# A two-layer graph kernel on one core: another order of work at the head, at the tail and in layer 1's first groups

## The chip, the core and the metric

The kernel runs on one core of a Trainium2 chip. The metric is the device time of the program in microseconds, as the median of several runs. One core has a matrix engine (TensorE, PE in the profile, with its weight loads as PEld), and three engines that work on tiles elementwise: VectorE (DVE), ScalarE (ACT) and GpSimd (POOL). SyncE (SP) issues most DMA transfers. Every engine has its own queue of instructions and takes them in program order; semaphores make one engine wait for another.

## The reference

All tensors are fp32; `x` is (64, 256, 512), that is 64 batches of 256 nodes with 512 features, and `adj` is (256, 256).

```python
def _layernorm(x):                     # no scale, no shift, eps 1e-5
    return (x - mean(x)) / sqrt(var(x) + 1e-5)

# layer 0
h = maximum(_layernorm(x), 0)
x = x + einsum('nm,bmd->bnd', adj, h) @ W0 + b0
# layer 1
h = maximum(_layernorm(x), 0)
q, k, v = (h @ W + b for W, b in ((Wq, bq), (Wk, bk), (Wv, bv)))    # 8 heads of 64
scores = q . k / 8 + (1 - adj) * -1e9                                # per batch and head, 256 x 256
out = softmax(scores) . v
x = x + out @ Wo + bo
```

## The kernel before

**Groups and layers.** The 64 batches are 32 groups of two. Layer 0 runs over all groups first (about 43 to 605 us of the profiled execution) and leaves the residual x and the transposed hidden tensor of every group in DRAM. Layer 1 runs over the groups again (about 605 to 2630 us, some 62 us for a group).

**Seven products for eight.** A matrix product is cut into 2x2 blocks and made with seven block products in Strassen's way (Winograd's form). Each operand needs four sums of blocks: on the weight side s1 to s4, on the data side t1 to t4 (`Halves.sums`, L483, on POOL: t1 = b12-b11, t3 = b22-b12, t2 = b22-t1, t4 = b21-t2). `project` is the one-level form: seven steps with the products a11.b11 (bank pa), a12.b21 (pb), s2.t2 (pa), s3.t3 (pc), s1.t1 (pa), a22.t4 (pc) and s4.b22 (pa). DVE adds the banks into the result (`add`, L802). Layer 0 uses it, and so do groups 0 and 1 of layer 1. From `FIRST2 = 2` on layer 1 uses `quartered`, in which most of the seven products (named A to G) are cut once more into seven. That needs sums of the sums: of the weights once (`block_sums`, which puts 128x128 sums of some 0.3 to 0.5 us on DVE or POOL, spread over ticks), of the data in each group (`Blocks.sums`, L582, on POOL).

**The order is written by hand.** A scheduler does not choose: instructions go into the engines' queues in the order in which the Python code emits them. A counter of ticks stands in for time. `after(delay, fn)` puts work off until `tick()` has been called so many times, and `run(gen, steps)` takes steps from a generator and ticks after each. `quartered` only makes a table of named steps, and an order string (QK, VO, V1, O1, OL) says how they follow: a token is the matrix (q, k, v, o), the product (A to G) and the step. Small letters are matmuls, copies and adds of one product; `oEk` is a matmul of wo's E and `oEl` the add after it. `|` is a tick, and `x` emits the next waiting exponent. QK makes q and k, VO makes v of the next group and the output of this one. V1 makes v alone and is used for groups 2 and 31; O1 makes the output of group 30, beside group 31's attention, and OL that of group 31.

**Layer 0's parts.** `ready(g, ...)` makes h: `moments` on DVE (L42, L43), `norm_scales` on POOL (L51 to L54: epsilon, power -1/2, and nb = -mean times it), relu on ACT (L830) with rs and nb as scale and bias. `turn_adjacency` transposes the adjacency: DVE copies it to another order of rows (adj_p, L362), PE transposes (L367), DVE copies the result to adjT. `first_adjacency` is group 0's adj.h in plain products (py, L856), copied by ACT to yT (L864) with POOL's t sums of `YH[0]` behind the copies; `adjacency(g)` is that of the other groups in the one-level form (py_a, py_b, py_c at L907, copies on ACT such as L926). It needs sums of adjT (`adjacency_sums`) and of h (`feature_sums`, L891, and `last_feature_sum`, L894, on POOL). `layer0(g)` multiplies by W0 (w_0a and so on, L490), adds to x, and makes the hidden tensor. `weight_sums` (L458) makes s1 to s4 of a weight.

**Layer 1's parts.** A seed is a copy by ACT of a bias or mask into a PSUM bank, on which PE then accumulates (`bank(seed=...)`, L291): the score banks are seeded with the mask, the output banks with the bias. `score` emits two seeded and two unseeded pairs of banks for each half of the heads; DVE reads them (L1126 seeded, L1129 unseeded), for the unseeded ones the row maximum is subtracted on POOL (L1136) or DVE (L1134), ACT takes the exponent in place (L1152), and POOL adds each pair of key tiles (`key_sum`, L1159). `attend` makes the denominators from those sums (pden, L1168) and attention times v (pav, L1175). The denominator is copied (L1182) and inverted by two ACT and three POOL instructions (L1189 to L1193), and in the last attention by DVE's reciprocal (L1197). `divide` (L1211) follows one tick later, then the t sums of the output and `block_outputs`. q and k leave PSUM by ACT copies (L1044). `outputs` issues the DMA of a finished batch (L1084), or in the last group of a quarter (L1082).

**The head and the tail.** The head is emitted as `ready(0)`, `load(1)`, `ready(1)`, a tick, `turn_adjacency`, sums of W0, and `first_adjacency`, of which three steps run before layer 0's seeds. At the tail of group 31 stand in this order: `attend(31, 0)`, `score(31, 1)`, six segments of O1, `attend(31, 1)`, the rest of O1, and OL.

Of the kernel before, what the change touches and what calls it, by code (L numbers as in the profile page):

```python
# [8 lines left out]
F32 = mybir.dt.float32  # L9
# [4 lines left out]
P = 128  # L14
# [31 lines left out]
def norm_scales(nc, pool, mhalf, mv, name):  # L46
# [8 lines left out]
    return rs, nb  # L55


def general_path(tc, x, adj, w0, b0, wq, bq, wk, bk, wv, bv, wo, bo, out):
# [157 lines left out]
    "vFa vA0 vFb vA1 vFc vFd x vA2 | vA3 vGa vFe vBa vp00 vBb vFf vGb | vCa vBc vFi vFg vCb vGc x vBd vFh vFj vCc "  # L216
    "vFl vEa | vBe vGd vEb vCd vGe vBf vCe vEc vCf vBn vGf vBg vEd vFk vGg | vCg vEe vBh vGh vp10 vBi vEf2 vBj x "
    "vCh vCi vDa vBk vGi | vDb vGj vp11 vGk vCj vGl vCk vEf x vDc vDd vm11 vDi | vDj vEg vDe vDk vDf vEi vCl vEj "
    "vEk vm10 vDg vEl0 | vEh vEl1 vDh vEl2 ")
O1 = (  # L220
    "oAz oCi oCj oCk oA0 oBz oA1 x oFa | oB0 oCa oFb oA2 oFc x oA3 | oFd op00 oB1 oFe oEa oCl0 oFf oFi oFg oFj | "
    "oEb oFk oCb oB2 oFh oFl oCc x oB3 op10 oEc | oEd oDa op11 oCd oG0 oCe oDb oG1 oCf oG2 | oEe x oEf oDc oG3 "
    "oCl1 oDi om11 oDj oDd | oCg oDe oEg oDf oDk oEi oCh oEj om10 oEk oDg | oEl oDh oEh ")
OL = (
    "oAz oBz oA0 oA1 oA2 | oA3 oB0 oB1 oFa op00 | oCi oFb oCa oCj oCb oCk oFc oCl0 oFd oEa oFe oCc | oCl1 oCd oEb "
    "oFf oCe oFi oCf oFg oFj oFk oEc oFh oCg oFl oEd | oDa oB2 op10 oB3 oDb oEe oG0 oCh oDc | op11 oDd oG1 oDe "
    "oG2 oDf oEf oG3 oDg | om11 oDi oDj oDk oDh oEg oEi om10 oEj oEk oEh | oEl ")
# [3 lines left out]
def kernel(  # L231
# [127 lines left out]
    def turn_adjacency():  # L359
        adj_p = tmp.tile([P, NT, N], F32, tag="u", name="adj_p")  # L360
        for u in range(NT):
            nc.vector.tensor_copy(adj_p[:, u, :].rearrange("p (t i b) -> p i t b", i=NI, t=NT),  # L362
                                  adj_r[:, u, :].rearrange("p (i t b) -> p i t b", i=NI, t=NT))
# [5 lines left out]
        nc.vector.tensor_copy(adjT, pa)  # L369
# [180 lines left out]
    def block_sums(n):  # L550

        todo = []
        for x in SMALL[n]:
# [5 lines left out]
            eng = nc.vector if x in "BFG" else nc.gpsimd  # L559
# [24 lines left out]
    def quartered(g, n, halves, blocks, by_token, place, first, seeds=None, multiplied=None, done=None):  # L584
# [160 lines left out]
        def more(name, b, i, k):  # L745
            step(name, lambda: add(place(i, k), banks[b], place(i, k)), b, quadrant=(i, k))
# [30 lines left out]
        if first is None:  # L777
            more("El", "pa", 0, 1)
# [35 lines left out]

    def ready(g, moments_at, scales_at, relus_at, batches=1):
# [7 lines left out]
        def scales(i):  # L823
            h.append(norm_scales(nc, small, mhalf, mv[:, i * n:(i + 1) * n, :], f"0_{g}_{i}"))
            if i == 0:
                H0[g] = act.tile([P, T, D], F32, tag="h", name=f"h_{g}", bufs=2)
# [20 lines left out]
    def first_adjacency():  # L847
# [4 lines left out]
        def part(d, b):  # L852
            if d not in pss:
                pss[d] = bank([P, GN], f"py_{d}")
            for k in range(NT):
# [3 lines left out]
        for d in range(DC):  # L859
            part(d, 0)  # L860
        for d in range(DC):
# [5 lines left out]
            if d == 3:  # L867
                YH[0].sums(nc.gpsimd, ("t3", "t4"))
# [13 lines left out]
    def feature_sums(g):  # L882
# [6 lines left out]
        for o, p, q, op in ((s12[:, 0], block(2, 1), block(2, 2), ALU.add), (s12[:, 1], s12[:, 0], block(1, 1), ALU.subtract),  # L889
                            (block(2, 1), block(1, 1), block(2, 1), ALU.subtract)):  # L890
            nc.gpsimd.tensor_tensor(o, p, q, op=op)  # L891
# [133 lines left out]
    def block_outputs(g, step):  # L1025
# [4 lines left out]
        if g == NG - 1:  # L1030
            both.sums(nc.vector)
# [42 lines left out]
    def outputs(g):  # L1074
# [4 lines left out]
        def done(i, k):  # L1079
            complete.append(k)  # L1080
            if g == NG - 1:
# [6 lines left out]
    def plain_outputs(g):  # L1088
        seeds = seed_outputs(g)
# [10 lines left out]
    def score(g, qd, sum_delay=5, exps=(3, 4, 5, 8)):  # L1100
# [4 lines left out]
        def banks(c, b, **how):  # L1105
            return [bank([P, NT * N], f"sc_{g}_{qd}_{c}{b}_{j}", **how) for j in range(2)]

        masked = {cb: banks(*cb, seed=maskT_f, times=1.0 / SCALE) for cb in ((0, 0), (0, 1))}
        while behind_seeds:
            behind_seeds.pop(0)()  # L1110
        for c in range(2):
            for b in range(GB):
                seen = (c, b) in masked
                ps = masked[c, b] if seen else banks(c, b)
# [46 lines left out]
    def attend(g, qd):  # L1161
# [47 lines left out]
        def divide():  # L1209
# [12 lines left out]
            if qd and g >= FIRST2:  # L1222
                block_outputs(g, 1)
# [186 lines left out]
```

## Time and profile before

| what | us |
|---|---|
| median of 3 runs | 2631.18 |
| the 3 runs | 2628.93 to 2632.58 |
| the profiled execution: its time | 2632.4 |
| its span, from the first to the last instruction | 2630.2 |
| busy in the span: PE | 2588.6 (98%) |
| PE weight loads | 2301.6 (88%) |
| POOL | 2075.6 (79%) |
| DVE | 1909.8 (73%) |
| ACT | 1379.4 (52%) |

A busy row is the sum of an engine's instructions in the profiled execution. The page cuts the span into 40 slices of 65.8 us, and PE's row there shows 7 in the first and the last slice and 9 in all between. The granted clock, PEclk, is the speed of TensorE as a part of its full speed; its mean over the span is 0.997. A busy microsecond at clock 0.50 does half a microsecond's work. A matmul of fp32 is a row with "f32" behind its tile, and "out<-in" gives the tiles by the program's names.

### The profile page before, as it was taken

Reading aid. Unit: us, or ns where it says so; the run is one execution under the profiler, and the core shown is the slowest. Engines: PE = TensorE matmul, PEld = TensorE weight load, DVE = VectorE, ACT = ScalarE, POOL = GpSimd, SP = SyncE. Lnnn points to the kernel's source line nnn. Section 1 sums busy time; section 2 is a strip of 40 time slices with the busy share of each in tenths; the row PEclk is TensorE's granted clock in tenths of the full one; section 3 lists DMA queues with packets and bytes.
Section 4 is the critical chain, followed back from the end, with each engine's and each line's share of the span. In section 5 each row is a group of like instructions: output and inputs, shape, how many; then the busy total and the mean of one; then the engine's idle time right before and its main releaser. Section 6 shows DMA issues by size and latency. Waiting matters only on the chain. (4 is left out here: it accounts for less than half of the span.)

```text
span 2630.2 us, 57376 instructions
## 1 busy us (share of the span) xinstructions
PE 2588.6 (98%) x21876; PEld 2301.6 (88%) x21876; DVE 1909.8 (73%) x4166; ACT 1379.4 (52%) x3192; POOL 2075.6 (79%) x2256
## 2 busy tenths in 40 slices
PE   7999999999999999999999999999999999999997
PEld 6999899998788888888888888888888888888885
DVE  5878788875476767777777777777767777777776
ACT  3444454543455555555555555555555555555552
POOL 6888887783777888888877888888888888877884
PEclk9999999999999999999999999999999999999998
DMA  5776666664111122211111111111122211111101
GB/s 134 200 194 186 171 165 186 164 165 106 33 49 49 49 65 63 67 50 49 49 49 50 49 49 49 49 49 49 50 67 65 65 49 49 49 49 49 49 34 50
DMA packets 281095, 211.40 MB, mean 80 GB/s; under 512 B 145904, under 2 KB 212976, under 8 KB 280816
## 3 DMA queue, kind: packets, MB, share of 16 engines
q1 hardware_dynamic: 280352, 207.15, 29.7%
q8 instruction: 175, 2.87, 0.4%
q14 instruction: 104, 0.85, 0.1%
q10 hardware_dynamic: 464, 0.52, 0.1%
HBM read 106.96 MB, written 100.66 MB: 79 GB/s over the span
## 5 line engine op out<-in xcount | busy, mean ns | idle before, releaser
L1126 DVE SCALAR_TENSOR_TENSOR a<-sc,top 128x512 f32<-128x512 f32 x256 | 159.1, 684 | 271.6 <-PE sc L1118 259.1
L1136 POOL TENSOR_TENSOR a<-a,top 128x1024 f32<-128x1024 f32 x125 | 293.5, 2369 | 40.3 <-DVE a L1129 40.3
L1159 POOL TENSOR_TENSOR as<-a 128x512 f32<-128x512 f32 x256 | 318.3, 1276 | 5.8 <-ACT a L1152 5.8
L1191 POOL TENSOR_TENSOR as<-as 128x512 f32<-128x512 f32 x63 | 80.2, 1273 | 284.3 <-ACT as L1190 278.9
L1152 ACT ACTIVATE a<-a 128x1024 f32<-128x1024 f32 x256 | 271.7, 1063 | 15.3 <-POOL a L1136 15.3
L1118 PE MATMUL sc<-q,k 64*128 64x256 f32 x2048 | 240.1, 383 | 1.4 <-ACT sc L291 1.4
L1118 PEld LDWEIGHTS sc<-q,k 64*128 64x128 f32 x2048 | 196.7, 186 | 45.4 <-issue 25.1
L1175 PE MATMUL pav<-a,v 128*32 128x256 f32 x4096 | 234.6, 380 | 0.0
L1175 PEld LDWEIGHTS pav<-a,v 128*32 128x32 f32 x4096 | 133.4, 110 | 89.1 <-issue 1.3
L1182 ACT ACTIVATE as<-pden 128x512 f32<-128x512 f32 x64 | 38.3, 599 | 294.6 <-PE pden L1168 294.6
L42 DVE BATCH_NORM_STATS2 st<-x 128x6 f32<-128x512 f32 x256 | 173.1, 676 | 10.3 <-DMA x<-in_x_dram 8.1
L1129 DVE SCALAR_TENSOR_TENSOR a<-sc,maskT 128x512 f32<-128x512 f32 x256 | 158.4, 681 | 0.0
L291 ACT ACTIVATE sc<-maskT 128x512 f32<-128x512 f32 x256 | 137.4, 591 | 0.0
L830 ACT ACTIVATE h<-x,nb,rs 128x512 f32<-128x512 f32 x128 | 93.9, 803 | 76.8 <-POOL nb L54 76.8
L957 ACT ACTIVATE h<-x,nb,rs 128x512 f32<-128x512 f32 x128 | 97.2, 807 | 53.4 <-POOL nb L54 50.2
L891 POOL TENSOR_TENSOR hs<-h 128x512 f32<-128x512 f32 x31 | 39.4, 1270 | 73.8 <-ACT h L830 63.7
L483 POOL TENSOR_TENSOR t_o<-oT,t_o 128x512 f32<-128x512 f32 x63 | 80.5, 1279 | 12.1 <-DVE t_o L483 9.6
L1211 DVE TENSOR_TENSOR oT<-pav,as 128x512 f32<-128x512 f32 x128 | 82.1, 683 | 8.4 <-POOL as L1193 8.4
L582 POOL TENSOR_TENSOR spare<-h1T,spare 128x128 f32<-128x128 f32 x180 | 82.4, 458 | 7.1
L1044 ACT ACTIVATE q<-q_pa,bq_c 128x256 f32<-128x256 f32 (+1 forms) x150 | 61.8, 456 | 48.9 <-PE q_pa L633 36.6
L802 DVE TENSOR_TENSOR x<-o_pa,x 128x512 f32<-128x512 f32 x120 | 82.4, 687 | 6.1 <-PE o_pa L647 4.8
L52 POOL TENSOR_TENSOR rs<-rs,mhalf 128x2 f32<-128x2 f32 (+1 forms) x97 | 80.0, 825 | 8.1
(1639 smaller groups left out, 8736.1 us busy)
## 6 DMA issues: line engine op xcount, KB each, us to landing
x<-in_x_dram SPq DMA_DIRECT2D x256, 128.0 KB, 3.0
residual<-x SPq DMA_DIRECT2D x256, 128.0 KB, 2.4
hidden<-r SPq DMA_DIRECT2D x128, 256.0 KB, 4.4
h1T<-hidden SPq DMA_DIRECT2D x64, 512.0 KB, 7.4
x<-residual SPq DMA_DIRECT2D x32, 1024.0 KB, 7.8
out_dram<-x SPq DMA_DIRECT2D x62, 512.0 KB, 4.1
w_sb<-in_L_gnn_weight_dram SPq DMA_DIRECT2D x1, 1024.0 KB, 7.3
wq_sb<-in_L_gnn_Wq_dram SPq DMA_DIRECT2D x1, 1024.0 KB, 7.5
```

Source lines behind the costliest of these rows:

```text
L42: nc.vector.bn_stats(st, src)
L291: nc.scalar.mul(t, seed, times)
L582: eng.tensor_tensor(self.operand(o), self.operand(p), self.operand(q), op=ALU.subtract)
L830: nc.scalar.activation(H0[g][:, t, :], xt[:, t, :], AF.Relu, bias=nb[:, t % n:t % n + 1], scale=rs[:, t % n:t % n + 1])
L957: nc.scalar.activation(h1[:, k * NT + t, :], xt[:, k * NT + t, :], AF.Relu, bias=nb[:, t:t + 1], scale=rs[:, t:t + 1])
L1118: nc.tensor.matmul(ps[j][:, kt * N:(kt + 1) * N], k[j * HD:(j + 1) * HD, c, kt * P:(kt + 1) * P], q[j * HD:(j + 1) * HD, c, :], start=(kt ...
L1126: nc.vector.scalar_tensor_tensor(o, ps[j].rearrange("p (k n) -> p k n", k=NT), SCALE, top_b[:, 0:NT, :], op0=ALU.mult, op1=ALU.subtract)
L1129: nc.vector.scalar_tensor_tensor(o.rearrange("p k n -> p (k n)"), ps[j], SCALE, maskT_f, op0=ALU.mult, op1=ALU.add)
L1136: nc.gpsimd.tensor_tensor(a, a, top_b, op=ALU.subtract)
L1152: nc.scalar.activation(a, a, AF.Exp)
L1159: nc.gpsimd.tensor_tensor(AS[c, b], a4[:, :, 0, :], a4[:, :, 1, :], op=ALU.add)
L1175: nc.tensor.matmul(po[f][h * 32:(h + 1) * 32, b * N:(b + 1) * N], v[:, k, h * HD + f * 32:h * HD + f * 32 + 32], A[h // 2, b][:, (h % 2) * ...
```

## The change

The arithmetic is the same but for one inversion (below); what differs is where instructions stand, which engine does some of them, and how a few are cut.

1. **Head.** `turn_adjacency` is emitted first, with its copies on ACT. Group 0's h is made tile by tile (`first_ready`): epsilon on DVE and the power on POOL (`power`), nb in one DVE instruction (`shift`), the relu of a tile one tile behind. Group 1 uses `power` and `shift` too, at tick 8 instead of 4, with its relus at 9. `adjacency_sums` moves from tick 4 to 1, and group 1's feature sums from 8 to 9. `first_adjacency` runs over k first for batch 0, and t3 and t4 of `YH[0]` come one tick later. Group 2's relus come at 4 instead of 3.
2. **Feature sums.** In every group of layer 0 the third sum (s3, in place in h) is emitted before the second (s2).
3. **Seeds.** The seeds of group 0's first scores and those of the outputs of groups 0 and 1 are emitted before the last step of the product ahead of them.
4. **Block sums of weights.** wo's are all on POOL, and before wo's F was on DVE; wv's start at tick 3 instead of 2, two to a tick instead of four.
5. **Orders.** V1, O1 and OL are rewritten, and four segments of O1 instead of six stand ahead of `attend(31, 1)`.
6. **Tail.** The output sums of (30, 1) come six ticks later and those of (31, 0) four, behind key sums. Key sums and exponents of group 31 are due at other ticks, and POOL's subtraction in `score(31, 1)` comes three ticks later. In the last attention DVE takes half of the reciprocals and the ACT and POOL form takes the other half. t3, t2 and t4 of the last output are on DVE, both of its block sums on POOL. The last add is in two pieces, and the last quarter leaves by two DMAs, on SP's and ACT's queues.

```diff
+def power(nc, pool, mhalf, mv, name):
+    n = mv.shape[1]
+    rs = pool.tile([P, n], F32, tag="rs", name=f"rs_{name}")
+    nc.vector.tensor_scalar(rs, mv[:, :, 1], EPS, None, op0=ALU.add)
+    nc.gpsimd.tensor_tensor(rs, rs, mhalf[:, :n], op=ALU.pow)
+    return rs
+def shift(nc, pool, mv, rs, name):
+    nb = pool.tile([P, mv.shape[1]], F32, tag="nb", name=f"nb_{name}")
+    nc.vector.scalar_tensor_tensor(nb, mv[:, :, 0], -1.0, rs, op0=ALU.mult, op1=ALU.mult)
+    return nb
XX...
     def turn_adjacency():
-            nc.vector.tensor_copy(adj_p[:, u, :].rearrange("p (t i b) -> p i t b", i=NI, t=NT),
-                                  adj_r[:, u, :].rearrange("p (i t b) -> p i t b", i=NI, t=NT))
+            nc.scalar.copy(adj_p[:, u, :].rearrange("p (t i b) -> p i t b", i=NI, t=NT),
+                           adj_r[:, u, :].rearrange("p (i t b) -> p i t b", i=NI, t=NT))
...
-        nc.vector.tensor_copy(adjT, pa)
+        nc.scalar.copy(adjT, pa)
...
     def block_sums(n):
-            eng = nc.vector if x in "BFG" else nc.gpsimd
+            eng = nc.vector if x in "BFG" and n != "o" else nc.gpsimd
...
-            more("El", "pa", 0, 1)
+            more("El", "pa", 0, 1, 2 if g == NG - 1 else 1)
...
+    def first_ready():
+        xt, mv = X[0], small.tile([P, T, 2], F32, tag="mv", name="mv0_0")
+        H0[0] = act.tile([P, T, D], F32, tag="h", name="h_0", bufs=2)
+        rs = []
+        def relu(t):
+            nb = shift(nc, small, mv[:, t:t + 1, :], rs[t], f"0_0_{t}")
+            nc.scalar.activation(H0[0][:, t, :], xt[:, t, :], AF.Relu, bias=nb, scale=rs[t])
+        for t in range(T):
+            moments(nc, small, mv, t, xt[:, t, :], "0_0")
+            rs.append(power(nc, small, mhalf, mv[:, t:t + 1, :], f"0_0_{t}"))
+            if t:
+                relu(t - 1)
+        relu(T - 1)
...
     def ready(g, moments_at, scales_at, relus_at, batches=1):
-            h.append(norm_scales(nc, small, mhalf, mv[:, i * n:(i + 1) * n, :], f"0_{g}_{i}"))
+            if g == 1:
+                rs = power(nc, small, mhalf, part, name)
+                h.append((rs, shift(nc, small, part, rs, name)))
+            else:
+                h.append(norm_scales(nc, small, mhalf, part, name))
...
     def first_adjacency():
-        for d in range(DC):
-            part(d, 0)
+        for k in range(NT):
+            for d in range(DC):
+                part(d, 0, (k,))
...
-                YH[0].sums(nc.gpsimd, ("t3", "t4"))
+                after(1, YH[0].sums, nc.gpsimd, ("t3", "t4"))
...
     def feature_sums(g):
-        for o, p, q, op in ((s12[:, 0], block(2, 1), block(2, 2), ALU.add), (s12[:, 1], s12[:, 0], block(1, 1), ALU.subtract),
-                            (block(2, 1), block(1, 1), block(2, 1), ALU.subtract)):
+        for o, p, q, op in ((s12[:, 0], block(2, 1), block(2, 2), ALU.add),
+                            (block(2, 1), block(1, 1), block(2, 1), ALU.subtract),
+                            (s12[:, 1], s12[:, 0], block(1, 1), ALU.subtract)):
...
     def block_outputs(g, step):
-            both.sums(nc.vector)
+            both.sums(nc.gpsimd)
...
         def done(i, k):
-            if g == NG - 1:
+            if g == NG - 1 and (i, k) == (0, 1):
+                for t, queue in enumerate((nc.sync, nc.scalar)):
+                    queue.dma_start(quarter_of(out[g * GB + k], i)[:, t], quarter(xt, i, k)[:, t])
+            elif g == NG - 1:
...
+    def score_bank(g, qd, c, b, **how):
+        return [bank([P, NT * N], f"sc_{g}_{qd}_{c}{b}_{j}", **how) for j in range(2)]
+    def score_seeds(g, qd):
+        return {cb: score_bank(g, qd, *cb, seed=maskT_f, times=1.0 / SCALE) for cb in ((0, 0), (0, 1))}
-    def score(g, qd, sum_delay=5, exps=(3, 4, 5, 8)):
+    def score(g, qd, sums=(5, 6, 7, 8), exps=(3, 4, 5, 8), masked=None, top_at=0):
...
+                    elif top_at:
+                        after(top_at, lambda a: nc.gpsimd.tensor_tensor(a, a, top_b, op=ALU.subtract), a)
...
-        def invert():
+        def invert(c=slice(0, GN)):                  # the same five instructions on the columns c
...
         if final:
-            for c in range(4):
+            for c in range(2):
                 nc.vector.reciprocal(rden[:, c * P:(c + 1) * P], den[:, c * P:(c + 1) * P])
+            invert(slice(N, GN))
...
-            if qd == 0:
-                HO[g].sums(nc.gpsimd, ("t1",))
-            elif g < NG - 1:
-                HO[g].sums(nc.gpsimd, ("t3", "t2", "t4"))
+            late = 6 if (g, qd) == (NG - 2, 1) else 4 if (g, qd) == (NG - 1, 0) else 0
+            which = ("t3", "t2", "t4") if qd else ("t1",)
+            if late:
+                after(late, HO[g].sums, nc.gpsimd, which)
             else:
-                HO[g].sums(nc.vector, ("t3", "t2"))
-                HO[g].sums(nc.gpsimd, ("t4",))
+                HO[g].sums(nc.vector if final else nc.gpsimd, which)
             if qd and g >= FIRST2:
-                block_outputs(g, 1)
+                block_outputs(g, late + 1)
...
-    ready(0, (0, 0, 2, 2), (0, 2), (1, 1, 3, 3), batches=2)
+    turn_adjacency()
+    first_ready()
     load(1)
-    ready(1, (4, 4, 4, 4), (4,), (8, 8, 8, 8))
-    after(4, adjacency_sums)
-    after(8, feature_sums, 1)
-    after(8, last_feature_sum, 1)
+    ready(1, (4, 4, 4, 4), (8,), (9, 9, 9, 9))
+    after(1, adjacency_sums)
+    after(9, feature_sums, 1)
+    after(9, last_feature_sum, 1)
     tick()
-    turn_adjacency()
...
-            ready(g + 2, (1, 1, 1, 1), (1,), (3, 3, 3, 3))
+            ready(g + 2, (1, 1, 1, 1), (1,), (3, 3, 3, 3) if g else (4, 4, 4, 4))
...
-    run(plain(0, *second))
-    score(0, 0, 4, (3, 4, 5, 6))
+    second = plain(0, *second)
+    run(second, 6)
+    seeds = score_seeds(0, 0)
+    run(second)
+    score(0, 0, (4, 5, 6, 7), (3, 4, 5, 6), seeds)
...
-            score(g, 1, 3, (3, 4, 5, 6))
+            score(g, 1, (2, 3, 5, 4), (1, 2, 4, 3), top_at=3)
...
-        for n, at in (("q", 7), ("k", 16)) if g == 0 else (("v", 2),) if g == 1 else (("o", 2),) if g == 2 else ():
+        for n, at in (("q", 7), ("k", 16)) if g == 0 else (("v", 3),) if g == 1 else (("o", 2),) if g == 2 else ():
-                after(at + i // 4, *work)
+                after(at + i // (2 if n == "v" else 4), *work)
...
-            run(last, 6)
+            run(last, 4)
...
-            score(g + 1, 0, 5, None if g + 1 >= FIRST2 else (3, 4, 5, 8))
+            score(g + 1, 0, (5, 6, 7, 8) if g + 1 < NG - 1 else (1, 1, 1, 1), None if g + 1 >= FIRST2 else (3, 4, 5, 8))
...
-                run(plain(g + 1, n, halves, *rest))
+                steps = plain(g + 1, n, halves, *rest)
+                run(steps, 5)
+                seeds = seed_outputs(g)
+                run(steps)
                 multiplied()
...
-                    run(follow(steps, V1))
+                    steps = follow(steps, V1)
+                    run(steps, 6)
+                    if g < FIRST2:
+                        seeds = seed_outputs(g)
+                    run(steps)
```

## The prediction, made before the changed kernel ran

> **What bounds the kernel now.** I read the page's slices first, then the windows, then the waits of TensorE (PE), then the timeline around each wait. The windows (us: length, then busy time of PE, weight load, DVE, ACT, POOL, then the granted clock) say where PE is not busy:
>
> ```profile
> 0.00:50.00 50.00, 32.70 (x168) 27.68 (x169) 24.38 (x54) 17.00 (x27) 28.11 (x45) 1.00 0.55 134
> 50.00:600.00 550.00, 550.00 (x3341) 503.76 (x3340) 447.54 (x891) 266.72 (x413) 443.32 (x603) 1.00 0.67 177
> ...
> 640.00:820.00 180.00, 172.58 (x1335) 145.13 (x1334) 106.52 (x207) 84.48 (x195) 132.70 (x145) 0.99 0.20 51
> 820.00:2560.00 1740.00, 1740.00 (x16414) 1548.44 (x16413) 1263.13 (x2880) 975.94 (x2486) 1420.29 (x1410) 1.00 0.19 52
> 2560.00:2630.20 70.20, 54.08 (x448) 43.02 (x446) 47.00 (x99) 22.04 (x48) 35.75 (x31) 0.90 0.13 47
> ```
>
> PE is the bound: it has no idle in two stretches of together 2290 us. Its 41.6 us without work are 17.3 at the head, 0.8 between the layers, 7.4 in layer 1's first groups and 16.1 at the tail. Only there can an order of work bring anything. Who is waited for:
>
> ```profile
> PE pa L367 <- DVE adj_p L362: 10.0, 1, 10.0
> PE pden L1168 <- POOL as L1159: 5.1, 2, 3.7
> PE o_pb L633 <- DVE x L802: 3.8, 1, 3.8
> PE py_1a L907 <- ACT yT L926: 2.5, 1, 2.5
> PE o_0a L490 <- ACT o_0a L291: 2.2, 1, 2.2
> PE py_1c L907 <- POOL h L891: 2.1, 1, 2.1
> PE q_pb L633 <- DVE q_F L802: 1.7, 1, 1.7
> PE sc L1118 <- ACT sc L291: 1.4, 1, 1.4
> ...
> PE w_0a L490 <- POOL t_y L483: 1.1, 1, 1.1
> ```
>
> A wait costs more than itself where the clock falls after it. Windows of PE alone (busy, clock), after the wait at 712.40 and after those from 2572.30 on:
>
> ```profile
> 715.48:718.90 3.42, 3.42 (x10) 0.50 0.00 0
> ...
> 2576.00:2579.40 3.40, 2.03 (x12) 0.50 0.08 31
> 2579.40:2582.57 3.17, 3.03 (x32) 0.50 0.02 5
> ```
>
> At half clock a busy us does half a us of work. So 715.48 to 718.90 loses 1.7, 2576 to 2582.57 loses half of 5.06, 2.5. After the 3.8 wait, 2613.83 to 2616.40 is again at 0.50: 1.3. In all 5.5 us of lost work hide in "busy" time.
>
> **The change part by part** (losses are against the profiled execution: span 2630.2, its time 2632.4, 1.2 above the median of 2631.18).
>
> *Head.* Before, DVE copies adj_p only after the moments of two tiles of x; PE starts at 10.05, its first product (py) at 12.43 and ends py at 21.23. Now ACT makes adj_p and adjT. adj_r has landed by 5.9, ACT is free from 3.1; copies of 128x256 and 128x512 take it 0.37 and 0.59, the four transposes 1.1 (row L367): adjT stands at 8.6, hidden by the wait for x. The chain of tile 0: x ready 7.91, moments 0.7+0.2, epsilon on DVE (new, 128x1; the nearest row, L1369, is 0.15), POOL pow of 128x1 (0.72 for 128x2 and 1.03 for 128x4, so about 0.55), nb on DVE behind tile 1's moments, done at 10.05, relu 0.8: first product at 10.9, 1.5 earlier. Tile 1's nb stands behind tile 2's moments, whose x lands at 10.4, so relu 1 ends at 12.4; relu 3 ends at 14.2. With k outermost PE first does four matmuls on tile 0 alone, 3.4 at the cold spacing of 0.43 (0.217 warm); none of these waits. Of py's 32 records, 7.0 warm plus 2.4 for the cold start, the end is 20.3. The clock came to full at 15.75 before; an earlier start need not move that.
>
> What comes behind: yT's last copy at 21.7 (behind two seeds on ACT), POOL's t2 until 22.4 (the four adjT sums of 0.46 now lie ahead, beside py), then pow of group 1 (1.03) and only then nb on DVE at 23.7. This is a new wait: behind nb DVE holds the w_sb sum (0.66) and x<-w_0a (0.69), and PE's second use of w_0a waits for the latter: 25.15 instead of 26.35. Group 1's relus end at 26.7; POOL now makes h second, at 29.3, just under PE's 29.55, instead of third behind t3 and t4 at 33.2: the wait of 2.1 goes. L926 no longer stands behind relu(2) on ACT: the 2.5 goes. py_1a at 40.45 comes at 34.2 to 34.6. **6.1** (between 4.5, cold until 17.7, and 7).
>
> *Feature sums in the other groups.* Swapped on POOL, 1.27 each. Cover: in group 15 the three end by 306.0 and PE takes h at 313.1, s2 at 315.7. Zero; s2 would have to be 9 us later to count.
>
> *Seeds.* Those of score, o_0 and o_1 go ahead of the last product's copies. ACT is idle there (4.77 before 641.44, 3.58 before 712.44, 1.38 before 782.02), 0.54 to 0.6 each, and other banks are free. Behind the four score seeds waits L1044 of k, at 641.44 in any case. Saved: 1.35, 2.2 plus the 1.7 of clock, 0.6. **5.85** (4 to 6).
>
> *wv and wo block sums.* q_F stood behind four DVE sums, of which the first two took 1.35 and 2.32 against 0.28 in quiet, because POOL's L1136 of 2.37 ran. Two stay ahead of q_F; only 0.6 of the 1.7 goes. The waits at 750.2 and 752.1 (0.8) go with F and G moved; moved sums of 0.85 a pair may bring 0.1 to 0.3 four times. wo's F goes to POOL: 4 x 0.46, key sums end at 827.7 instead of 825.84 where PE reaches pden at 826.84, but POOL's last sums meet pden's last matmuls; I take 0.3 off the 0.65 gained. **1.3** (0 to 2.5).
>
> *V1.* New order in two groups; one wait of 0.4 goes, an unknown one may come. 0 (+1 to -1).
>
> *Tail.* V1 of group 31 ends at 2572.3. Key sums now stand ahead of eleven output sums on POOL: last exponent 2569.2, last key sum 2570.4; pden runs at once, 1.07+3.55 for both. Scores from 2577.05 (3.65; their seeds 2.9 after pden, 0.7 in hand). POOL's output sums (3x1.28+8x0.75 = 9.85) end 2580.25, and oCk at 2581.1 needs the last. From there POOL carries the end: the inversion (3.2) to 2583.4, two key sums 2.5, the top subtraction 2.4, two key sums 2.5: 2590.8. DVE: eight score reads to 2583.2, division to 2584.75, L1134 to 2585.95; exp on ACT to 2587.05, and the o_F copy queued behind it holds oFf until 2587.35 (reached at 2585). Four segments of O1 instead of six come before attention, so pden is reached at 2590.0 and waits for POOL. Whether L1134 or POOL's key sum goes first the trace does not tell (POOL's t_o took 2.19 beside L1134 against 1.28); the Trainium skill ("SBUF — State Buffer", "SBUF: two separate sides") has the first hold the shared ports for its whole instruction: 2590.8 or 2592.1. I take 2591.5; pav ends 2595.8. Then Da, G, Dc, Dd (2.4), and oEg waits for Ee, which DVE has behind the division and three sums (1.28+2.06, from 2597.1) at 2600.7: a wait of 2.5. The reciprocal's other half on ACT and POOL (about 2.5) ends before pav. Rest of O1 to 2602.85; OL 11.5 of work (12 matmuls of 0.43, 28 of 0.22) and 1 of small waits, its block sums on POOL (to 2602.5) just ahead: 2615.3 against 2624.75. The last add in halves and two queues: 5.2 after it instead of 5.45. Gain 9.7.
>
> Here a rule must be weighed. **The row**: 2.18 of idle at 712.40 brought half clock; 2.49 at 37.95 did not. **The rule** ("TensorE: Matmul & The Clock Gate", "Part 1: The HAM clock gate"): the clock halves after a whole idle window of about 3.4 us. By the rule none of the new waits (2.1, 1.5, 2.5) throttles: 9.7. By the row each may, 1.7 apiece: 4.6 if all three do. I follow the row with less than one such loss: **8.5** (4.5 to 10).
>
> Sum: 6.1+5.85+1.3+8.5 = 21.75; 0.5 for waits not found: 21.2. Of the execution 2632.4-21.2 = 2611.2, of the median 2610.0.
>
> **The rivals.** *More:* the tail loses no clock and the block sums no wait: 25, 2606. *Less:* the tail moves its waits to POOL and throttles twice, the head gains 4.5: 15, 2616. For it: POOL has 20 us in a row from 2570.4 to 2590.8. *Same:* the starts are earlier and everything ends at the next transfer or POOL sum: under 5. Against it: the middle has 2290 us without one idle us, so a lead once won is kept. *Slower:* layer 0's POOL. h and s2 swap in 30 groups and POOL is busy 443 of 550 there; if s2 came late at py_a, up to 1.27 per group, 38 in all, would be lost: net 17 slower, about 2648. It decides from 0.9 per group (26.5 us: the gain and the 5.3 of the bound). Against it: s2 has 9 us in hand.
>
> **How the numbers follow.** Likeliest case 0.62 (2606 to 2614), More 0.14, Less 0.18, Same 0.03, Slower 0.03. About what a measurement can tell from no change is 0.2%, 5.3 us. Leaving out half of More's low end and the two last cases: 2604 to 2617. Faster 0.94, same 0.03, slower 0.03.
>
> **What would show it.** Right: first py near 11; no PE wait on as L1159 over 2 us for group 31's first half; clock 1.00 around 715; py_1a's wait on ACT gone; a PE wait on DVE in O1 behind attention. Wrong: PE idle between 50 and 600 or 820 and 2560; q_F's wait gone wholly; clock 0.50 twice behind 2580; under 4 gained before 50 us.

## The result and the profile after

| | median, us | its runs | before, same chip | ratio, 95% interval |
|---|---|---|---|---|
| changed kernel | 2617.72 | 2616.85 to 2618.1 (4) | 2631.88 | 0.9946 [0.9928, 0.9963] |

The change gains 14.2 us; 21.2 were forecast, and 2617.72 lies 0.7 above the range. The profiled execution took 2618.1, its span is 2616.3 (before 2630.2). The windows of the changed kernel, in the columns shown before (length, then busy PE, weight load, DVE, ACT, POOL; granted clock):

```profile
0.00:50.00 50.00, 37.89 (x198) 32.73 (x199) 31.72 (x72) 22.14 (x34) 29.87 (x45) 1.00 0.54 137
50.00:600.00 550.00, 548.89 (x3317) 501.42 (x3316) 445.69 (x879) 263.77 (x411) 440.93 (x598) 1.00 0.67 177
...
640.00:820.00 180.00, 177.43 (x1421) 150.66 (x1424) 112.03 (x221) 86.63 (x205) 139.96 (x155) 1.00 0.19 49
820.00:2560.00 1740.00, 1739.92 (x16392) 1550.05 (x16385) 1263.92 (x2877) 977.48 (x2490) 1420.30 (x1407) 1.00 0.19 52
2560.00:2616.30 56.30, 43.95 (x380) 35.83 (x378) 35.27 (x78) 15.62 (x35) 31.14 (x33) 0.91 0.16 58
```

PE now works 37.9 of the first 50 us (32.7 before) and 177.4 of 180 in layer 1's first groups (172.6). The tail still has 12.4 us without PE and a clock of 0.91. Its waits (total, times, longest):

```profile
PE pa L382 <- ACT adj_p L377: 6.5, 1, 6.5
PE o_Fs L648 <- ACT o_F L685: 2.9, 1, 2.9
PE py L897 <- ACT h L842: 2.8, 1, 2.8
PE o_Es L648 <- DVE x L821: 2.8, 1, 2.8
PE w_0a L505 <- DVE x L821: 1.7, 1, 1.7
PE q_pb L648 <- DVE q_F L821: 1.4, 1, 1.4
PE pden L1218 <- POOL as L1209: 1.4, 2, 0.8
PE w_1a L505 <- POOL t_y L498: 0.7, 1, 0.7
```

The waits for feature sums, for yT's copy, for the seeds and, at 2572, for key sums are gone. Four are new (o_Fs, o_Es, w_0a for DVE, w_1a); the first three were forecast.

Waits don't show where the gain went. The start of the same matmul in both kernels does (us, from the timelines; "lead" is before minus after; w_Na is the first product of group N in layer 0, and (31, 1) the second half of the heads in group 31):

| PE starts | before | after | lead |
|---|---|---|---|
| w_1a (layer 0, group 1) | 46.69 | 41.08 | 5.61 |
| w_2a | 65.03 | 60.34 | 4.68 |
| w_31a | 603.43 | 602.18 | 1.26 |
| scores of (0, 0) | 642.82 | 640.07 | 2.75 |
| pden of (1, 0) | 728.56 | 720.99 | 7.57 |
| scores of (3, 0), in the group behind the wo sums | 831.29 | 822.91 | 8.38 |
| scores of (31, 0) | 2556.43 | 2547.15 | 9.28 |
| scores of (31, 1) | 2585.09 | 2567.24 | 17.85 |
| pden of (31, 1) | 2599.75 | 2583.14 | 16.61 |
| last matmul's end | 2624.75 | 2610.42 | 14.33 |
| end of the span | 2630.18 | 2616.32 | 13.86 |

Two losses stand out: 4.35 of the head's 5.61 us are gone at the end of layer 0, and 4 of the 17.85 between the last scores and the end.

### The profile page after: what moved, and what is told of

Same layout as the page of the kernel before. It is cut to its first block, busy times and chain, and to the rows that moved or that the text cites. A ratio compares the mean times of both kernels' runs of the same rounds, so it can differ in the third digit from the quotient of the medians.

```text
span 2616.3 us, 57383 instructions
## 1 busy us (share of the span) xinstructions
PE 2587.3 (99%) x21876; PEld 2304.1 (88%) x21876; DVE 1910.3 (73%) x4165; ACT 1379.8 (53%) x3198; POOL 2077.2 (79%) x2259
## 4 chain that ended last, share of the span: by engine, by line
PE 88%; POOL 5%; DVE 4%; DMA 2%; issue 1%; SPq 1%; ACT 1%; DVEq 0%; ACTq 0%; POOLq 0%
PE sc L1166 9%; PE pav L1225 8%; PE o_pa L662 4%; PE pden L1218 2%; PE v_pa L648 2%; PE q_pa L648 2%; PE k_pa L648 2%; PE v_pa L662 2%; PE o_pc L662 2%; PE q_pa L662 2%; PE k_pa L662 2%; PE o_pa L648 2%; PE v_pc L648 1%; PE q_pc L648 1%; PE k_pc L648 1%; DVE st L42 1%
## 5 line engine op out<-in xcount | busy, mean ns | idle before, releaser
L1242 POOL TENSOR_TENSOR as<-as 128x512 f32<-128x512 f32 x64 | 80.9, 1264 | 275.1 <-ACT as L1241 264.3
L821 DVE TENSOR_TENSOR x<-o_pa,x 128x512 f32<-128x512 f32 (+1 forms) x121 | 82.4, 682 | 9.0 <-PE o_pa L662 5.2
L1244 POOL TENSOR_TENSOR as<-as 128x512 f32<-128x512 f32 x64 | 81.0, 1265 | 5.4
L498 POOL TENSOR_TENSOR t_y<-yT,t_y 128x512 f32<-128x512 f32 (+1 forms) x65 | 82.2, 1265 | 3.4 <-ACT yT L906 1.0
```

## Experiments

All were timed against the kernel before on their own chip, whose median differs by up to 0.9 us; "gain" is that median minus theirs. Starts and waits are of their profiled executions. e2 and e7 edit the kernel before, e3 and e4 the changed kernel. e5, e6, e8, e10 and e11 edit e1's kernel, e9 that of e8, and e12 puts e1, e6, e9, e10 and e11 together.

| run | median | gain | ratio, 95% interval |
|---|---|---|---|
| e1_swap_group1 | 2615.36 | 18.0 | 0.9938 [0.9924, 0.9951] |
| e2_swap_alone | 2638.49 | -5.2 | 1.0020 [1.0011, 1.0029] |
| e3_epsilon_on_dve | 2618.84 | 14.5 | 0.9948 [0.9935, 0.9962] |
| e4_sums_on_dve | 2618.51 | 14.8 | 0.9951 [0.9937, 0.9965] |
| e5_t3_behind_scales | 2666.85 | -33.3 | 1.0129 [1.0113, 1.0144] |
| e6_e_sums_before_division | 2614.77 | 18.8 | 0.9928 [0.9915, 0.9942] |
| e7_seeds_alone | 2627.63 | 6.0 | 0.9979 [0.9972, 0.9987] |
| e8_key_sums_own_tiles | 2615.29 | 18.3 | 0.9932 [0.9919, 0.9946] |
| e9_short_pool_chain | 2612.93 | 19.8 | 0.9922 [0.9909, 0.9936] |
| e10_t4_behind_scales | 2614.55 | 18.2 | 0.9931 [0.9917, 0.9944] |
| e11_last_dma_whole | 2615.21 | 17.5 | 0.9936 [0.9922, 0.9949] |
| e12_together | 2610.72 | 22.0 | 0.9913 [0.9900, 0.9927] |

### Who sets layer 0's pace: e1, e2, e3, e5, e10

The suspicion came from PE's starts in layer 0: groups at 18.69 us in the changed kernel, 18.57 in the kernel before, and 18.34 in both where nothing presses. First the new order of the feature sums, for group 1 alone in the changed kernel (e1) and by itself in the kernel before (e2); in shorthand:

```diff
-        for o, p, q, op in (s1, s3, s2):
+        for o, p, q, op in (s1, s3, s2) if g == 1 else (s1, s2, s3):
```

> The changed kernel with one edit: the new order of the feature sums (s1, s3, s2) for group 1 alone, the old one (s1, s2, s3) for all groups after it. Theory A: in layer 0 the changed kernel is bound by POOL's own loop of 18.69 us per group, against 18.57 in the kernel before, because in the new order two sums out of four start behind a sum that they read (0.12 more for the pair s2, s4). Then the loop is 18.57 again, the first product of w_31 comes about 2.9 us earlier (599.3 for 602.2), and the time is 2614.8. Rival B: the lead won at the head is lost in layer 0 for another reason (transfers, ACT), and the order of the sums costs nothing, as the prediction said: 2617.7, w_31 at 602.2.

> The kernel before with only the new order of the feature sums, in all groups. Theory A: POOL's loop in layer 0 goes from 18.57 to 18.69 us; 30 groups of it make the first product of w_31 about 3 us later, less what the earlier third sum saves at py_1c in the head (2.1): 2632 to 2635, with w_31 at 605 to 606 for 603.4. Rival B (no effect beyond the head): 2629.8, w_31 at 601.3.

e1: w_31a at 599.12, 3.06 earlier than in the changed kernel; theory A had 2.9. In the whole time the intervals of the two overlap, but the starts tell them apart: the five runs with e1's layer 0 (e1, e6, e8, e9, e11) have w_31a at 599.12 to 599.96, the two with that of the changed kernel (itself and e4) at 602.18 and 602.71. e2: w_31a at 608.12, 4.7 later than in the kernel before and 2 later than theory A had it. Of that 0.97 are there at w_1a, where theory A expected a gain: t3 and t4 of the head still stand ahead of the sums, and py_1a now waits 3.51. The other 3.7 come in layer 0. The order alone is a loss. POOL's timeline says why; first the changed kernel (start, length):

```profile
112.37 1.28 POOL L934 TENSOR_TENSOR hs<-h 128x512 f32<-128x512 f32 x1 [1.81 <-ACT h L871]
113.72 1.27 POOL L934 TENSOR_TENSOR h<-h 128x512 f32<-128x512 f32 x1
114.95 1.26 POOL L934 TENSOR_TENSOR hs<-hs,h 128x512 f32<-128x512 f32 x1
116.29 1.27 POOL L937 TENSOR_TENSOR hs<-h,hs 128x512 f32<-128x512 f32 x1
```

and e1, in the old order:

```profile
112.06 1.27 POOL L934 TENSOR_TENSOR hs<-h 128x512 f32<-128x512 f32 x1 [1.82 <-ACT h L871]
113.41 1.27 POOL L934 TENSOR_TENSOR hs<-hs,h 128x512 f32<-128x512 f32 x1
114.64 1.27 POOL L934 TENSOR_TENSOR h<-h 128x512 f32<-128x512 f32 x1
115.86 1.27 POOL L937 TENSOR_TENSOR hs<-h,hs 128x512 f32<-128x512 f32 x1
```

A sum that reads what the one before it wrote, or overwrites what that one reads, starts 1.34 or 1.35 behind it, another 1.22 or 1.23. The old order has one such step in the three, s1 to s2. The new one has two: s1 to s3 (which overwrites what s1 reads) and s2 to s4. That is 0.12 us. It counts because POOL runs in a loop with hardly a gap: its only idle time in this group, 1.81, is that in which ACT makes four relus from POOL's own nb. PE takes t3 (for w_3c and on) 0.05 us after POOL has made it in groups 3 to 13 and from 24 on; in the kernel before, in groups 6 to 13 and from 28 on. In between PE has more work of its own (the output bias's product at group 13 makes that group 3.7 us longer), and POOL gets ahead.

e3 takes work from POOL and gives DVE a little:

```diff
 def norm_scales(...):
-    nc.gpsimd.tensor_scalar(rs, mv[:, :, 1], EPS, None, op0=ALU.add)
+    nc.vector.tensor_scalar(rs, mv[:, :, 1], EPS, None, op0=ALU.add)
```

> The changed kernel with one edit: in norm_scales of every group the addition of epsilon (POOL, 0.22 us and a gap of 0.09, three times in a group) goes to DVE, directly behind the moments; DVE gets three short instructions. The order of the feature sums stays the new one. Theory A: POOL's loop falls from 18.69 to about 17.8 us, under the 18.34 that PE needs, so PE sets the pace of layer 0: the wait of w_Nc for POOL's t3 goes, the first product of w_31 comes at about 596.3 for 602.2, and the time is 2611.8. Rival B (transfers or DVE set the pace of layer 0, not POOL): 2617.7 or more, with the periods of 18.69 kept.

By its time rival B, but the groups now take 18.34 and some 18.8 us in turn, not 18.69. PE no longer waits for t3 (1.7 us or more in hand up to group 30), yet w_31a comes at 604.79. Now POOL waits for epsilon, which stands in DVE's queue behind adds, and PE for DVE's adds (0.15 to 0.88 in the groups that show it). The waits from 50 to 600 us:

```profile
POOL hs L934 <- ACT h L871: 66.7, 28, 3.0
POOL rs L52 <- DVE rs L51: 42.6, 57, 2.1
```

e5 and e10 touch POOL's order alone, from group 2 on: e5 puts t3 and t4, e10 only t4, behind the scales of the group after next, into the time in which POOL waits for the relus (in shorthand):

```diff
-        after(3, YH[g].sums, nc.gpsimd, ("t3", "t4"))
+        after(3, YH[g].sums, nc.gpsimd, ("t3",))                       # e5: this one late too
+        after(3 if g == 1 else 4, YH[g].sums, nc.gpsimd, ("t4",))
...
-            ready(g + 2, (1, 1, 1, 1), (1,), ...)
+            ready(g + 2, (.8, .8, .8, .8), (.9,), ...)                 # for g > 0: ahead of what is due at 1
```

> The kernel of e1_swap_group1 with one edit in layer 0: from group 2 on POOL makes rs and nb of the group after next ahead of the sums t3 and t4, not behind them, so that the 2.9 us in which ACT makes the four relus from nb lie beside t3 and t4 (2.5 us) instead of an idle POOL. Nothing moves on DVE. Theory A: POOL's loop of 18.57 us is its own work plus that idle time; it falls to about 16.3, PE sets the pace at 18.34, w_31 comes at about 596.4 for 599.1 and the time is 2.7 lower than e1's (2612.6 where e1 has 2615.4). Rival B: DVE is next at the same pace, as e3_epsilon_on_dve showed when DVE got three short instructions more (periods of 18.8 in every second group): no gain. Rival C: t3, now 1.7 us later in the loop, makes PE wait in each group: slower.

> The kernel of e1_swap_group1 with one edit in layer 0: from group 2 on only the sum t4, not t3, stands behind rs and nb of the group after next on POOL, in the idle time in which ACT makes the four relus. t3, for which PE waits, keeps its place. Theory A: POOL's loop of 18.57 falls by 1.2 to about 17.3, PE sets the pace at 18.34, w_31 comes at about 596.6 for 599.1: 2.5 lower than e1. Rival B: scales that stand 1.2 earlier wait for DVE's moments, as they did in e5_t3_behind_scales (2.3 us there), and the loop does not shrink: as e1 or slower.

e5 is 51 us slower than e1 (rival C). The scales come so early that POOL waits for DVE's moments, and t3, for which PE waits, stands behind them. POOL in e5, 50 to 600 us:

```profile
POOL rs L51 <- DVE mv L43: 82.1, 53, 4.4
```

DVE's moments in turn wait behind adds of PE's products: the loop now goes through three engines, at 20.1 us a group. e10 leaves t3 where it was. PE's timeline in the changed kernel, e1 and e10, one fence each: the first number is the start of the first product of groups 9 and 10.

```profile
190.55 0.81 PE L505 MATMUL w_9a<-w_sb,yT 128*128 128x256 f32 x3
...
209.24 1.03 PE L505 MATMUL w_10a<-w_sb,yT 128*128 128x256 f32 x4
```

```profile
189.78 1.67 PE L505 MATMUL w_9a<-w_sb,yT 128*128 128x256 f32 x7
...
208.37 1.89 PE L505 MATMUL w_10a<-w_sb,yT 128*128 128x256 f32 x8
```

```profile
189.42 1.89 PE L505 MATMUL w_9a<-w_sb,yT 128*128 128x256 f32 x8
...
207.76 1.89 PE L505 MATMUL w_10a<-w_sb,yT 128*128 128x256 f32 x8
```

18.69, 18.59 and 18.34: in e10 PE sets the pace, with t3 made 1.9 us or more ahead of its use from group 2 to 30, and w_31a at 596.99, 2.1 ahead of e1 (expected 2.5; 1.2 are lost once at w_1c, since in group 1 the scales stand ahead of t3 too). The whole gains only 0.8, less than the intervals can tell. Of the 2.1 in the traces 1.3 are gone before the scores of (31, 0), in the middle, where executions differ by as much (below). The tail takes back 0.4: no half clock falls behind o_Fs, so PE reaches pden of (31, 1) 1.6 earlier (counted from the scores), but it waits 2.34 there for POOL instead of 0.76, with a half clock behind it.

### The seeds: e7

```diff
+    run(second, 6)
+    seeds = score_seeds(0, 0)
+    run(second)
+    score(0, 0, 4, (3, 4, 5, 6), seeds)
...
+                run(steps, 5)                 # group 1; group 2 alike, after six segments of V1
+                seeds = seed_outputs(g)
+                run(steps)
```

> The kernel before with only the seeds of the first scores and of the outputs of groups 0 and 1 emitted before the last step of the product ahead of them. Theory A: the three waits go (1.42, 2.18, 0.64), and so does the half clock behind the second (1.7): 5.9 lower than the kernel before, clock 1.00 from 712 to 722. Rival B: the half clock there has another cause than the wait: 4.2 lower, with 0.50 still in a window near 712. Rival C: the seeds' reads of maskT and of the bias on ACT hold back the copies of the last product: under 3.

6.0, where theory A had 5.9. The interval (3.4 to 7.4 us) does not exclude rival B's 4.2, but the clock does. The clock in e7 (window length, busy PE, clock), where the kernel before had 0.50 for 3.4 us:

```profile
710.40:713.80 3.40, 3.40 (x18) 1.00 0.00 0
713.80:717.20 3.40, 3.40 (x17) 1.00 0.00 0
```

### The tail: e4, e8, e6, e9, e11, e12

> The changed kernel with one edit in the tail: the three output sums of (30, 1) that stand on POOL behind group 31's first key sums (3.9 us, from 2561.6) go to DVE, which has no work from 2564.3 to 2568.5. Theory A: POOL's chain (output sums, inversion, division on DVE, key sums, subtraction, key sums) sets when the last attention can start; without 3.9 us of it the wait of o_Fs for ACT falls from 2.9 to about 1.4 and loses its clock penalty, POOL's last key sum ends 1.7 us earlier, and the time is 2616.0. Rival B: the new wait of pden for POOL is 2.7 us long and brings the half clock itself: 2617.7. Rival C (POOL's chain has slack and DVE pays): slower by up to 1.

```diff
-                after(late, HO[g].sums, nc.gpsimd, which)
+                after(late, HO[g].sums, nc.vector if qd else nc.gpsimd, which)
```

From the scores of (31, 1) to pden of (31, 1) e4 takes 12.7 us for 15.9, and to the end of that attention 20.1 for 21.8, so POOL's chain does carry that stretch. But the sums stand in DVE's queue ahead of V1's last adds, and v_Es waits 1.40 for these; pden of (31, 1) then waits 2.33. No half clock falls in e4's tail, and still the gain is as the changed kernel's; its profiled execution came to the scores of (31, 0) 1.7 us later, and v_Es makes it 3.4 at those of (31, 1).

What holds POOL is in the changed kernel's timeline, POOL first, then ACT:

```profile
2573.64 1.27 POOL L1244 TENSOR_TENSOR as<-as 128x512 f32<-128x512 f32 x1
2576.39 3.32 POOL L1209 TENSOR_TENSOR as<-a 128x512 f32<-128x512 f32 x2 [1.49 <-DVE oT L1263]
2579.67 2.35 POOL L1184 TENSOR_TENSOR a<-a,top 128x1024 f32<-128x1024 f32 x1
2581.99 2.50 POOL L1209 TENSOR_TENSOR as<-a 128x512 f32<-128x512 f32 x2
...
2577.45 1.06 ACT L1202 ACTIVATE a<-a 128x1024 f32<-128x1024 f32 x1 [3.91 <-DVE a L1182]
2578.41 0.25 ACT L685 COPY o_F<-o_Fs 128x128 f32<-128x128 f32 x1
```

The key sums wait 1.49 for DVE's division: they go into the tile (`AS["all"]`) in which the denominators lie that it divides by. Then they meet DVE's L1182 and take 3.32 for 2.50. And the copy o_F, for which PE waits 2.9, stands in ACT's queue behind an exponent that waits for the same L1182.

> The kernel of e1_swap_group1 with one edit in the tail: the key sums of (31, 1) go to tiles of their own (those of the queries and keys of (31, 0), which nobody reads any more), and no longer to the tile in which the denominators of (31, 0) lie until DVE has divided by them. Theory A: POOL waits there 1.5 us for that division and then works beside DVE's subtraction (3.3 for 2.5); without it the last key sum ends 1.4 earlier, the wait of the last pden for POOL (0.76) goes, and no more, since PE itself comes no earlier because of the wait of o_Fs: 0.8 lower than e1. Rival B: the wait is on the exponents, not on the tile: as e1.

```diff
+        if (g, qd) == (NG - 1, 1):
+            AS[c, b] = act.tile([P, 2, N], F32, tag=f"{'qk'[c]}0{b}", ...)
...
```

The waits for the division and of pden are gone (theory A), and next to nothing is won (a gain of 18.3 for e1's 18.0; theory A had 0.8): POOL's second key sum now holds up L1182 (2.29 for 1.22), and this in turn POOL's subtraction (3.35 for 2.35). The exponent comes later, and o_Fs waits 3.94.

> The kernel of e1_swap_group1 with one edit in O1: the two adds out of o_Es (oEe, oEf), which stand on DVE behind the last division and the three sums t3, t2, t4, go ahead of the last attention, where DVE has nothing to do for 4.3 us. Theory A: the wait of o_Es for DVE (2.80 us) goes and with it the half clock behind it (1.7); PE reaches OL 4.5 us earlier and then waits about 1.2 for POOL's block sums and up to 0.8 for the next ones: 2.5 lower than e1 (2612.9 where e1 has 2615.4). Rival B: POOL's block sums, not DVE's order, set OL; OL starts earlier and ends where it did: as e1.

```diff
...
-oFl oB2 oB3 | op10 oDa op11 oG0 oDb oG1 oCe oCf | oG2 oEe oG3 oEf
+oFl oB2 oB3 oEe oEf | op10 oDa op11 oG0 oDb oG1 oCe oCf | oG2 oG3
...
```

The wait of 2.80 goes, and one of 1.85 for DVE's next add (o_pa) comes, with a half clock behind it as before. From the last pav to PE's end it is 20.5 for e1's 21.4: 0.9, nearer to rival B, though DVE and not POOL now holds PE up. DVE's division and three sums (3.4 us in a row) are ahead of every add there.

> The kernel of e8_key_sums_own_tiles (own tiles for the last key sums) with two edits more in the tail: the eight block sums of (30, 1) (6 us on POOL ahead of the inversion) go to DVE, behind the last adds of V1, where it has nothing to do for 4.2 us; and in O1 the ACT copy oFe stands directly behind oFc, ahead of the exponent that waits for DVE. Theory A: PE was held twice in the same stretch, by o_Fs for ACT (with a half clock behind it) and by POOL's chain, so that e8, which took away one of them, gained nothing before the last attention; with both gone pden of (31, 1) starts 4.5 earlier (counted from the scores of (31, 1)) and waits about 1.3 for POOL, and the time is 4 to 5 lower than e1's (2610.9 where e1 has 2615.4). Rival B: the DVE chain (score reads, division, subtraction) takes POOL's place: under 2 lower. Rival C: the half clock is the whole of it: 1.7 lower.

```diff
-            after(step, last.sums, nc.gpsimd)        # for (30, 1)
-            after(step, both.sums, nc.gpsimd)
+            behind_values.append(lambda: (last.sums(nc.vector), both.sums(nc.vector)))   # run behind V1
...
-oA2 oA3 oFb x oCa oEa oFc | oFd oB0 oEb oFe
+oA2 oA3 oFb x oCa oEa oFc oFe | oFd oB0 oEb
...
```

From the scores to pden of (31, 1) 12.9 us for e1's 15.9 and e8's 16.9, and to the end of that attention 18.9 for 21.8 and 21.4: one wait away gave 0.4, both 2.9. The waits of e9:

```profile
PE o_Es L648 <- DVE x L821: 2.8, 1, 2.8
...
PE pden L1224 <- POOL as L1215: 1.5, 2, 0.9
...
PE o_Fs L648 <- ACT o_F L685: 0.4, 1, 0.4
```

The median is 2.4 lower than e1's (1.8 by the gains), about half of what theory A gave. That execution came into the tail 2.4 us later than e1's (scores of (31, 0) at 2546.28 for 2543.93), which the edits don't explain, so the stretch is the better measure. Against e8 it makes two edits at once, which were not taken apart; e4 shows that fewer sums on POOL alone bring 1.7 in this stretch.

> The kernel of e1_swap_group1 with one edit at the very end: the last add in one piece and the last quarter by one DMA on SP's queue, as before the change. From PE's last matmul to the end of the span it was 5.43 in the kernel before and 5.90 in the changed one. Theory A: the split costs 0.5: 5.43 again, and the time is 0.5 lower than e1 (which a measurement of the whole cannot tell; the trace can). Rival B: the 5.9 come from the half clock or from where PE ends, and the split gains what the prediction said (0.25): 6.1.

From PE's end to the end 6.07, for 5.94 in e1: theory A's 5.43 did not come. With the new tail this stretch is 5.53 to 6.27 where the last DMA is split and 6.07 and 5.66 where it is whole (e11, e12), so the split is neither a loss nor a gain that can be seen. With the old tail (the kernel before, e2, e7) it is 5.30 to 5.43. Why it grew stays open.

> All edits that take a wait away together: e9's three in the tail, the adds out of o_Es ahead of the division (e6), t4 behind the scales in layer 0 (e10), the last DMA whole (e11), the new order of the feature sums for group 1 alone (e1). If each gives what it should by itself and they do not meet: 4.5 + 0.9 + 2.5 + 0.5 = 8.4 lower than e1, 2607.0 where e1 has 2615.4. If DVE becomes the bound in the tail once POOL is out of the way: 2610 to 2612.

2610.72, 4.6 below e1 (4.0 by the gains) and 22.0 below the kernel before; its interval lies below that of the changed kernel. w_31a comes at 597.55, pden of (31, 1) 12.9 behind the scores. o_pa's wait for DVE (1.86, with a half clock) is what stays: the second of the two cases that the expectation named.

## Why the prediction was wrong

Its sum against the profiled executions, in leads:

| step | forecast | measured |
|---|---|---|
| head | 6.1 | 5.6 |
| layer 0 | 0 | -4.35 |
| seeds | 5.85 | 6.9 |
| wv and wo sums | 1.3 | 0.2 |
| middle | 0 | 0.9 |
| tail | 8.5 | 4.6 |
| waits not found | -0.5 | - |

The lead at the end is 7.3 short of the forecast. Layer 0 (4.35) and the tail (3.9) are all of it; the other terms nearly cancel. Of the signs named, all five for the forecast came. Of those against it the clock fell twice in the tail (from 2578.65 and 2595.72), and "PE idle between 50 and 600" came as no more than 1.1 us.

**Head: right.** First py at 10.48 (10.9), w_0a's wait for nb's followers to 25.73 (25.15), py_1a and py_1c without waits. From w_1a to w_2a another 0.9 goes: the second use of w_1a waits 0.7 for t_y on POOL.

**Layer 0: the step that failed.** "A lead once won is kept", because PE had no idle time from 50 to 600, and "Zero" for the swapped sums with 9 us in hand. A busy row is no proof that PE sets the pace: matmul ends are modelled, and 550 of 550 us were "busy" at 18.57 a group, where PE's own work is 18.34. PE and POOL where PE takes t3 (yT) for w_8c in the kernel before, then PE alone in e10, where t3 is there in time:

```profile
183.35 1.06 PE L907 MATMUL py_9b<-adjT,h 128*128 128x128 f32 x8
183.06 1.28 POOL L483 TENSOR_TENSOR yT<-yT 128x512 f32<-128x512 f32 x1
184.40 1.13 PE L490 MATMUL w_8c<-w_sb,yT 128*128 128x256 f32 x4
```

```profile
178.94 1.06 PE L950 MATMUL py_9b<-adjT,h 128*128 128x128 f32 x8
179.83 1.03 PE L505 MATMUL w_8c<-w_sb,yT 128*128 128x256 f32 x4
```

w_8c starts 1.05 behind py_9b, 0.06 after t3 is made, where 0.89 would do, and no idle time is shown. The second matmul of w_8c starts another 0.1 late. The hand of 9 us was that of s2 ahead of PE; but the engine that was short was POOL, in which s2 is one step of a loop. And it was read in group 15, one of those where POOL is ahead (t3 stands there 2.6 us before its use): in groups 6 to 13 and from 28 on PE takes t3 as soon as it is made. POOL's 443 of 550 us do not speak against it: a good part of the rest is its wait for ACT's relus, which is part of the loop. The prediction's rival "Slower" had the place right and the mechanism wrong: not s2 late at py_a, but 0.12 more in POOL's loop, 3.06 in all (e1), and 1.3 that POOL takes back in the old order too, the 0.9 at w_1a among them (e1 keeps 4.3 of 5.6). Against e10, which lets PE set the pace, POOL's loop costs e1 another 2.1. e1, e2 and e10 edit nothing but the order on POOL.

**Seeds: right, mechanism and clock.** e7 alone gives 6.0, and 6.9 by the starts in its trace. A term was missing: the first scores took 4.03 us while their four seeds arrived one by one, and 3.35 when all were there (0.7).

**Weight sums: mis-sized.** q_F's wait went from 1.73 to 1.44, 0.3 for 0.6. Two waits at 750 went, but of the 1.5 won there 1.0 is lost again by the next pden. The key sums behind wo's sums make pden wait 0.6 at 818 and stretch it; 0.3 was taken off, and the lead falls by 1.36 there, from 9.74 to 8.38. No run took this part alone.

**Middle.** The 0.9 between 831 and 2547 is not the change's: it is between -0.3 and 1.1 in the other runs, kernels with and without the change. Its cause is not known.

**Tail: the order of events was right, four sizes were not.** Counted from the scores of (31, 1), POOL's last key sum was forecast at 14.45 and came at 17.25: the wait for the division (1.5) was missed, key sums behind L1182 took 0.8 more (of the two orders left open, DVE's instruction went first), and POOL began its output sums a us later in this count. Behind the last attention o_Es waited 2.8 (2.5), but the half clock behind it took 1.7. From PE's end to the end it was 5.9 for 5.2. OL was 0.6 shorter than forecast. In leads: 2.5 less than forecast at the end of the last attention, another 1.9 at PE's end, 0.7 at the end of the span, less the 1.2 that were taken off for the clock. The half clock behind o_Fs cost nothing by itself, since POOL was later still: in e10 none falls there, and the last pden starts 17.3 behind the scores, as in e1.

**The rule weighed.** By the row (a wait of 2.2 brought half clock) the tail was worth 4.6 if three waits throttle; by the Trainium skill ("TensorE: Matmul & The Clock Gate", "Part 1: The HAM clock gate"), a whole idle window, 9.7. The row was nearer: the clock halved behind two of the waits, o_Fs and o_Es, with 2.79 and 2.14 us of idle PE in a window of 3.41, not a whole one. That 4.6 was also measured is luck. Only the loss behind o_Es counted (1.7, where 1.2 had been taken off); most of the rest came from POOL's chain and from the last transfers.

## What to carry to other kernels

Compare the starts of the same matmul in both kernels over the whole span: a lead that shrinks in a stretch without idle time shows another engine's loop as the bound, and an instruction "with much in hand" still costs its time if it sits in that loop. When two queues hold the same consumer, taking one wait away shows little; follow both to what they share (here POOL's sums ahead of the inversion, for which DVE's division and, behind it, ACT's copy and POOL's key sums wait). Read what an instruction has in hand in the groups where it is least, not in one group. A tile reused for the next result is a wait for its last reader.

## What the runs showed of the hardware

**The clock fell behind a window of 3.41 us in which PE had been idle for about 2.** Changes of the granted clock lie on a grid of 3.41 us that starts with the first full clock (13.9 to 17.5 us in these executions): in the changed kernel it is full from 15.24, halves at 2578.65, 751 times 3.413 later, and again at 2595.72, 5 times 3.41 behind that. Its windows (length, busy PE, clock):

```profile
2575.24:2578.65 3.41, 0.62 (x3) 1.00 0.00 0
2578.65:2582.06 3.41, 3.35 (x15) 0.50 0.00 0
...
2592.31:2595.72 3.41, 1.27 (x11) 1.00 0.00 0
2595.72:2599.13 3.41, 3.41 (x17) 0.50 0.10 41
```

The same wait of 2.81 in e4, which the grid cuts in two:

```profile
2591.97:2595.38 3.41, 1.42 (x9) 1.00 0.00 0
2595.38:2598.79 3.41, 2.59 (x23) 1.00 0.00 0
```

Over the 14 profiled executions every window with 2.06 us or more of idle PE was followed by one at 0.50; none with 1.83 or less was, where it was itself at full clock; between 1.86 and 2.0 both happened. This settles the prediction's two cases in the kernel before: the wait at 712.40 lies in one window (2.18 idle of 3.41), that at 37.95 is cut in two (1.7 and 0.8). What a half window costs shows from the last pav to PE's end: 21.4 in the changed kernel, e1, e5 and e9, and 19.7 in e3, e4, e8, e10 and e11, which have the same wait of 2.8 for o_Es but no half clock behind it. So a wait of 2.2 to 3 us costs 1.6 to 1.7 more or not by where it falls, and that is a good part of what the tails of these runs differ by.

**Of a large sum on POOL and one on DVE, the one that began first kept its time, and the other was held up by about what was left of it.** The prediction reckoned with this. In the changed kernel L1182 of DVE began at 2576.14 and took its 1.22; the two key sums, begun at 2576.39 with 0.96 of it left, took 3.32 for 2.50. In e8 L1182 began at 2574.46, just behind a key sum with 1.21 left, and took 2.29; the key sum kept its 1.26. POOL's subtraction, begun at 2575.62 with 1.13 of L1182 left, took 3.35 for 2.35. Whether that holds for other kinds of instruction was not tried.
